# Graph convolution on one core: eight x quads loaded among the last segment's reads, and a table of gates for the scatters

## The chip, the cores and the metric

The kernel runs on one core of a Trainium2 chip. A core has TensorE (PE for its matmuls, PEld for its weight loads), VectorE (DVE), ScalarE (ACT), GpSimd (POOL) and SyncE (SP), which run side by side and wait for each other by semaphores, and 16 DMA engines that all queues share. Here SP issues the plain transfers and POOL the indirect ones, the scatters. The time is that of one execution on the device, in microseconds; lower is better.

## The reference

There are N = 12500 nodes with 128 features and 412500 edges (src, dst, 20 edge features, one weight), sorted by dst.

```python
h   = relu(layernorm(x)) @ W_in2f
Wij = (ssp(edge_attr @ W_f1 + b_f1) @ W_f2 + b_f2) * edge_weight[:, None]
agg = segment_sum(h[dst] * Wij, src, num_segments=N)     # ssp(x) = softplus(x) - log 2
out = x + ssp(agg @ W_o1 + b_o1) @ W_o2 + b_o2
```

The edges are sorted by the end that is read (dst), so the rows of h come from a narrow window; the sum goes by the other end (src), which is in random order.

## The kernel before

The edges are worked in 806 chunks of 512, that is four tiles of 128 edges each (`QT = 4`). A step of the main loop is one chunk, with the engines' parts of it staggered over several chunks. `hidden` (L710) multiplies the edge features by W_f1 on PE, ACT and DVE turn them into softplus values, `value` (L834) multiplies by W_f2 on PE, `window` and `pick` (L818, L846) pick the edges' rows of h out of their window by a 0/1 matrix, `blocks` and `rank` (L747, L766, L799, L771) work out a free slot for each edge, and `message` (L863, L864) writes the product and the edge's place in its node block into a buffer `o`. There are 16 such buffers (`BACK = 16`).

`scatter` (L873) then issues, on POOL, one indirect DMA for each of a chunk's four tiles, from `o` to a table `slots` in device memory. The chunks form seven segments, each with a table of its own. When a segment's chunks are scattered, `Collect` reads its table back (`load`, L919 on SP), compares places (`compare`, L932 on DVE, L938 on POOL), and sums by a matmul into `acc` (`add`, L953), and `keep` (L985, L987) adds `acc` to the nodes' sums `agg`. A unit is what one `load` reads. The first six segments' units are spread over later steps and over steps behind the last chunk; the seventh's are read at the end, together with the output stage `finish` (L443 to L460), which takes a quad (512 nodes) through two matmuls and adds x.

What sets the order: it is written out by hand, one queue per engine, in the order of the calls in `step(k, units)`. Three things tie the engines' paces. A buffer `o` is free again when its scatters of 16 chunks earlier have landed, so DVE's L863 waits for them. `behind` makes PE's matmuls of a step wait for the scatters of 16 chunks earlier. And `scatter(k, kept["v"])`, called behind `value(k + 1)`, gives the first scatter of chunk k-1 a wait for the last matmul of that `value`; this is the gate. Chunks before 24 (`PACED`) and the last 12 steps have no gate.

Of x, which `finish` adds to the result, 25 quads are loaded to SBUF ahead of the output stage. Eight come in the main loop (`x_early`). The other 17 (`x_late`: buffers xr, xf, xh and xm, 8, 4, 2 and 3 quads) are loaded on SP (L428) behind the sixth segment's last read and ahead of the seventh's first one, each with an addition of the bias on POOL (L433) that stands behind the last scatter.

Of the kernel before, what the change touches and what calls it, by code (L numbers as in the profile page):

```python
# [17 lines left out]
P = 128  # L18
# [27 lines left out]
def gnn_kernel(  # L46
# [498 lines left out]
    with tc.tile_pool(name="edge", bufs=2) as edge, tc.tile_pool(  # L545
# [57 lines left out]
        class Group:  # L603
# [101 lines left out]
            def hidden(self, c):  # L705

                z = psum.tile([P, 2, CH], F32, name="z")
                for k in range(2):
                    rows = slice(32 * (c + k), 32 * (c + k) + RBF)
                    mm = nc.tensor.matmul(z[:, k, :], wf1[rows, :], self.f[rows, :],  # L710
                                          start=True, stop=True)
                    if k == 1:
                        behind(mm, self.g * NCHUNK + c - LZ, 3)
                self.pair[c] = z

            def hidden_log(self, c):
# [36 lines left out]
            def rank(self, c):  # L753

                seg = self.seg
                if c == 0:
                    self.top = edge.tile([P, TG], F32, name="top")
                    self.slot = edge.tile([P, TG], I32, name="slot", bufs=8)
                k = self.g * NCHUNK + c
                if k > seg.c0:  # L760
                    self.pass_on()
                if k == seg.cleared and k > seg.c0:
                    used = self.used()
                    self.limit(6 * len(segs), ALU.is_gt, seg.low, used[:, :, :NBLK - 1])
                    self.limit(6 * len(segs) + 1, ALU.is_gt, seg.low_last, used[:, :, NBLK - 1:])
                nc.tensor.matmul(free, after, self.inb[c], start=k == seg.c0, stop=False,  # L766
                                 skip_group_check=True)
                kept["inb"] = self.inb[c]

            def rank_end(self, c):  # L770
# [58 lines left out]
            def value(self, c, v):  # L829

                r = self.pair[c // 2 * 2][:, c % 2, :]
                k = self.g * NCHUNK + c - 1
                for i in range(QT):
                    mm = nc.tensor.matmul(v[:, i, :], r[:, i * P:(i + 1) * P], wf2,  # L834
                                          start=False, stop=True, skip_group_check=True)
                    if i == 1:
                        behind(mm, k, k % 2)
                kept["v"] = mm
                return v

            def pick(self, c, at, ps):

                near = self.near.pop(c)
                k = self.g * NCHUNK + c - 2
                for i in range(QT):
                    mm = nc.tensor.matmul(ps[:, i, :], at[:, i * P:(i + 1) * P], near,  # L846
                                          start=i == 0, stop=i == QT - 1, skip_group_check=True)
                    if i == 1:
                        behind(mm, k, 2 + k % 2)

            def picked(self, c, ps):

# [11 lines left out]
                nc.vector.tensor_mul(o[:, :, :P], v, hg)  # L864
                self.o[c] = o

            def scatter(self, c, after=None):

                views = self.seg.views
                o = self.o.pop(c)  # L870
                for i in range(QT):
                    j = c * QT + i
                    put = nc.gpsimd.indirect_dma_start(  # L873
                        out=views[j % VIEWS],
# [2 lines left out]
                        in_offset=None,  # L877
                    )
                    puts.append(put.ins.name)
                    if i == 0 and after is not None:  # L880
# [13 lines left out]
        class Collect:  # L894
# [47 lines left out]
            def add(self, u):  # L942
                b0, nb, t0, nt = self.units[u]
                m, to = self.m.pop(u), self.to.pop(u)
                for j in range(nb * nt):
                    b, t = b0 + j // nt, t0 + j % nt
                    if b % QT == 0 and t == 0:
                        self.few = QT if "rest" in kept else 2
                    few = self.few
                    i = b % few  # L950
                    if i == 0 and t == 0:
                        self.acc[b // few] = self.room(b // few)
                    nc.tensor.matmul(self.acc[b // few][:, i, :], m[:, j, :P], to[:, j, :],  # L953
                                     start=t == 0, stop=t == self.seg.tiles(b) - 1)
# [93 lines left out]

        tops, ps = [], {}
        waiting = []  # L1050
        LAG, PACED = 1, 24

        def step(k, units=()):

# [11 lines left out]
            def message(k):  # L1066
                g, c = of(k)
                g.message(c, vs.pop(k), hgs.pop(k))
                waiting.append(k)
# [57 lines left out]
            for r in ready[-1:]:  # L1127
                next(r, None)
                tops.append(r)
            if k in HEAD:  # L1130
                part("end", made["log"] - 1, pairs(hidden_end))
            elif k != -1:
# [3 lines left out]
            for c, u in units:  # L1136
                if summed:
                    summed[0].add(summed[1])
                summed[:] = c, u

        zeros = {}
        units = {}
# [66 lines left out]
            return t.rearrange("p (c f) -> p c f", f=P)  # L1209

        xs = {}
        NX = 8

        def early_homes():
            for q in range(NX):
# [56 lines left out]
        with tc.manual_schedule():  # L1272
# [36 lines left out]
            x_late = x_ahead(late_homes(), nc.gpsimd, bo2)  # L1309
# [25 lines left out]
            nc.vector.tensor_copy(flag, worst)  # L1335
            for _ in x_early:
                pass
            for _ in x_late:
                pass


            last = collects[-1]
# [90 lines left out]
```

## Time and profile before

| | |
|---|---|
| median of 3 runs | 4208.53 us (4207.98 to 4208.92) |
| profiled execution | 4207.59 us, its span 4205.9 us |
| POOL busy in scatters | 3093.3 us, 3224 of 959 ns |
| POOL's idle time before scatters | 1011.8 us |
| first and last scatter start | 22.96 us, 4108.09 us |
| DVE's L863 waiting for scatters that land | 677.6 us |
| SP issues the 17 late quads of x | from 4100.85 us |
| SP issues the seventh segment's first read | 4119.62 us |
| DVE's first comparison of the seventh segment | 4123.84 us |

The profile names an operation by its line, engine and tiles (`out<-in`). Times of a timeline row are its start and its duration in us; in square brackets stands how long the engine was idle before it, and what ended that. In a group's row the numbers behind the bar are the sum of busy time in us, the mean duration of one in ns, and the idle time in front of them. "issue" is time in which an engine waited for nothing that the profile shows.

### The profile page before, as it was taken

To read this page: it belongs to the slowest core of one execution; us is meant where nothing else is said; L and a number is where in the kernel's file an instruction comes from. 1 tells how busy PE (TensorE), PEld (TensorE's weight loads), DVE (VectorE), ACT (ScalarE), POOL (GpSimd) and SP (SyncE) were. 2 spreads that over 40 slices of the span, in tenths; PEclk is the share of its full clock that TensorE was granted. 3 is DMA by queue.
4 is the path that set the end of the run, shared out by engine and by line. 5 is a ranking of instruction groups with operands and counts; after the bars stand their busy time and mean duration, and the time that the engine had idled before them with its cause. 6 is when DMAs were issued, how large, how long until landed. Compare 5 with 4: busy or idle time off the path is not lost. (4 is left out here: it accounts for less than half of the span.)

```text
span 4205.9 us, 68388 instructions
## 1 busy us (share of the span) xinstructions
PE 3305.9 (79%) x21594; PEld 2564.3 (61%) x21594; DVE 3134.5 (75%) x7192; ACT 2774.6 (66%) x5494; POOL 3137.6 (75%) x3298
## 2 busy tenths in 40 slices
PE   6777667676676666678888888988888888888887
PEld 4555445444444444457776776767777767667786
DVE  7887666666555555668877887888888888888986
ACT  6887676667666666666666666766666666666624
POOL 5777777777777777777777777777777777777774
PEclk8877776667766667679999998999999999999999
DMA  5776655655444354467778777778777977787776
GB/s 173 215 231 210 193 171 178 188 158 177 142 127 132 110 169 152 139 198 235 230 227 278 226 220 214 229 227 278 232 229 205 297 230 209 235 243 213 218 231 192
DMA packets 494767, 858.10 MB, mean 204 GB/s; under 512 B 141018, under 2 KB 276558, under 8 KB 494398
## 3 DMA queue, kind: packets, MB, share of 16 engines
q1 hardware_dynamic: 390798, 640.38, 52.1%
q0 software_dynamic: 103168, 213.15, 15.0%
q8 instruction: 174, 2.85, 0.3%
q14 instruction: 195, 1.60, 0.1%
q10 hardware_dynamic: 432, 0.13, 0.0%
HBM read 457.62 MB, written 395.69 MB: 203 GB/s over the span
## 5 line engine op out<-in xcount | busy, mean ns | idle before, releaser
L873 POOL DMA_INDIRECT slots<-o,slot x3224 | 3093.3, 959 | 1011.8 <-issue 720.4
L856 ACT ACTIVATE hg<-picked,rcut 128x128 f32<-128x128 f32 x3224 | 909.6, 364 | 409.5 <-PE picked L846 396.2
L834 PEld LDWEIGHTS v<-wf,r 128*128 128x128 f32 x6448 | 997.4, 233 | 252.4 <-issue 128.1
L834 PE MATMUL v<-wf,r 128*128 128x128 f32 x6448 | 1075.4, 321 | 24.2 <-ACT v L826 11.7
L953 PEld LDWEIGHTS acc<-to,m 128*128 128x128 f32 x5660 | 723.4, 205 | 213.4 <-DVE agg L987 87.6
L826 ACT ACTIVATE v<-bf 128x512 f32<-128x512 f32 x806 | 484.8, 601 | 535.2 <-DVE o L864 516.0
L710 PE MATMUL z<-f,wf 20*128 20x512 f32 x1612 | 564.5, 783 | 346.2 <-DVE r L742 343.9
L953 PE MATMUL acc<-to,m 128*128 128x128 f32 x5660 | 768.1, 293 | 71.0 <-DVE agg L987 51.1
L863 DVE COPY o<-place 128x4 f32<-128x4 f32 x806 | 151.8, 188 | 678.7 <-DMA slots<-o,slot 677.6
L932 DVE TENSOR_TENSOR to<-numbers,m 128x640 f32<-128x640 f32 (+3 forms) x793 | 629.7, 824 | 29.4 <-DMA m<-slots 19.7
L846 PE MATMUL picked<-near,at 126*128 126x128 bf16 x3224 | 363.7, 243 | 329.2 <-DVE o L864 322.8
L864 DVE TENSOR_TENSOR o<-v,hg 128x512 f32<-128x512 f32 x806 | 552.3, 685 | 80.3 <-PE v L834 75.1
L742 DVE SCALAR_TENSOR_TENSOR r<-z,nbf,a 128x1024 f32<-128x1024 f32 x402 | 512.8, 1276 | 81.3 <-ACT a L722 80.6
L846 PEld LDWEIGHTS <-at 126*128 126x128 bf16 x3224 | 290.5, 111 | 380.4 <-issue 310.7
L747 DVE TENSOR_TENSOR inb<-numbers,blk 128x392 f16<-128x392 f32 x806 | 446.1, 554 | 96.0 <-PE numbers L953 95.7
L719 ACT ACTIVATE a<-z,bf 128x1024 f32<-128x1024 f32 x402 | 442.4, 1101 | 113.8 <-PE z L710 113.5
L722 ACT ACTIVATE a<-a,half 128x1024 f32<-128x1024 f32 x402 | 461.6, 1148 | 13.1
L710 PEld LDWEIGHTS z<-f,wf 20*128 20x128 f32 x1612 | 142.3, 215 | 522.1 <-DVE r L742 493.2
L771 DVE TENSOR_REDUCE top<-free 128x4 f32<-128x392 f32 x806 | 446.1, 553 | 13.0 <-PE free L766 12.5
L720 ACT ACTIVATE a<-a 128x1024 f32<-128x1024 f32 x402 | 424.9, 1057 | 12.7
L953 PEld LDWEIGHTS numbers<-to,m 128*128 128x128 f32 x2492 | 326.7, 211 | 156.3 <-DVE to L932 145.2
L953 PE MATMUL numbers<-to,m 128*128 128x128 f32 x2492 | 354.9, 301 | 69.7 <-DVE to L932 68.8
(126 smaller groups left out, 1984.8 us busy)
## 6 DMA issues: line engine op xcount, KB each, us to landing
m<-slots SPq DMA_DIRECT2D x307, 387.0 KB
rel<-rel_d SPq DMA_DIRECT2D x202, 504.0 KB
m<-slots SPq DMA_DIRECT2D x278, 322.5 KB
f<-in_f_t SPq DMA_DIRECT2D x101, 512.0 KB
slots<-o,slot POOLq DMA_INDIRECT x3224
m<-slots SPq DMA_DIRECT2D x193, 258.0 KB
slots<-zero SPq DMA_DIRECT2D x96, 387.0 KB
slots<-zero SPq DMA_DIRECT2D x58, 516.0 KB
```

What stands on the lines that cost most here:

```text
L710: mm = nc.tensor.matmul(z[:, k, :], wf1[rows, :], self.f[rows, :], start=True, stop=True)
L722: nc.scalar.activation(a, a, AF.Ln, bias=half, scale=0.5)
L742: nc.vector.scalar_tensor_tensor(r, z, nbf1, a, op0=ALU.max, op1=ALU.add)
L747: nc.vector.tensor_tensor(inb, count_ps[:, None, :NBLK].to_broadcast([P, QT, NBLK]), self.blk[:, c * QT:(c + 1) * QT, None].to_broadcast([ ...
L826: nc.scalar.activation(v, spread(bf12, QT), AF.Copy)
L834: mm = nc.tensor.matmul(v[:, i, :], r[:, i * P:(i + 1) * P], wf2, start=False, stop=True, skip_group_check=True)
L846: mm = nc.tensor.matmul(ps[:, i, :], at[:, i * P:(i + 1) * P], near, start=i == 0, stop=i == QT - 1, skip_group_check=True)
L856: nc.scalar.activation(hg[:, i, :], ps[:, i, :], AF.Copy, scale=self.rcut[:, j:j + 1])
L864: nc.vector.tensor_mul(o[:, :, :P], v, hg)
L873: put = nc.gpsimd.indirect_dma_start(out=views[j % VIEWS], out_offset=bass.IndirectOffsetOnAxis(ap=self.slot[:, j:j + 1], axis=0), in_=o[: ...
L932: nc.vector.tensor_tensor(to[:, :n, :], count_ps[:, None, :].to_broadcast([P, n, P]), m[:, :n, P:].to_broadcast([P, n, P]), op=ALU.is_equal)
L953: nc.tensor.matmul(self.acc[b // few][:, i, :], m[:, j, :P], to[:, j, :], start=t == 0, stop=t == self.seg.tiles(b) - 1)
```

## The change

Three things are changed.

**The gates.** `STRETCH = 40` cuts the chunks into stretches of 40. For ten of the stretches a table `GATES` gives another gate than the one of before. `("v", 8)` and `("v", 12)` release two or three chunks' tiles together, at the `value` of a step one or two later. `("end", 4)` and `("end", 8)` release one or two chunks at the step's end, behind the last matmul that was issued in it, a collect's if there is one. `("each", 1)` releases one tile at each of four points of a step: behind `value`, `pick`, `rank` and at the end. To have that matmul, `kept["mm"]` takes each newest one. All other stretches gate as before.

**The front.** In stretches 12 and 16 (`FRONT`) the units' comparisons stand at the front of a step, ahead of `message`, and no longer behind `blocks`.

**The late x.** Nine of the 17 late quads are loaded and biased as before (`NOW = 9`: the eight xr and the first xf). The other eight (three xf, two xh, three xm, the last of them only 212 rows) are loaded on SP behind the seventh segment's reads of units 6, 8, 10 and so on, and get their bias on POOL three units later.

```diff
+        LAG, PACED, STRETCH = 1, 24, 40
+        GATES = {2: ("v", 2 * QT), 3: ("each", 1), 5: ("end", QT), 6: ("v", 3 * QT),
+                 7: ("v", 2 * QT),
...
+        FRONT = (12, 16)
...
-            def scatter(k, after=None):
-                while waiting and (waiting[0] < PACED or k >= NCH - PACED // 2
-                                   or after is not None and waiting[0] <= k - LAG):
-                    j = waiting.pop(0)
-                    g, c = of(j)
-                    g.scatter(c, after if j >= PACED and k < NCH - PACED // 2 else None)
-
+            def scatter(k, point=None):
+                while waiting:
+                    j, i = waiting[0]
+                    if j < PACED or k >= NCH - PACED // 2:
+                        n, after = QT - i, None
+                    else:
+                        where, n = GATES.get(j // STRETCH, ("v", QT))
+                        n = min(n, ((j // STRETCH + 1) * STRETCH - j) * QT - i)
+                        if point not in (("v", "pick", "rank", "end") if where == "each" else (where,)):
+                            return
+                        if j * QT + i + n > (k - LAG + 1) * QT:
+                            return
+                        after = kept["mm"]
+                    while n > 0:
+                        j, i = waiting.pop(0)
+                        g, c = of(j)
+                        e = min(QT, i + n)
+                        g.scatter(c, range(i, e), after)
+                        after = None
+                        n -= e - i
+                    if e < QT:
+                        waiting.insert(0, (j, e))
+                        return
+
+            front = 0 <= k < NCH and k // STRETCH in FRONT
+            for c, u in units if front else ():
+                c.compare(u)
             if k in vs:
                 message(k)
...
-                    scatter(k, kept["v"])
+                    scatter(k, "v")
...
                 g.pick(c, ats.pop(k + 2), ps[k + 2])
+                scatter(k, "pick")
...
             for c, u in units:
-                c.compare(u)
+                if not front:
+                    c.compare(u)
...
+            for w in late[:NOW]:
+                x_load(*w)
+            for w in late[:NOW]:
+                x_bias(*w, nc.gpsimd, bo2)
...
             for u in range(len(last.units)):
                 last.load(u + 5)
+                i = NOW + u // 2
+                if u % 2 and i < len(late):
+                    x_load(*late[i])
+                if not u % 2 and NOW <= i - 2 < len(late):
+                    x_bias(*late[i - 2], nc.gpsimd, bo2)
```

The order of the instructions shows the change at three places.

The SP queue behind the sixth segment's last read, before; `slots_122` is the seventh segment's table, and a row ends with the count of such instructions in a row:

```order
L428 DMA xr<-in_x 128x4x128 x8
L428 DMA xf<-in_x 128x4x128 x4
L428 DMA xh<-in_x 128x4x128 x2
L428 DMA xm<-in_x 128x4x128 x2
L428 DMA xm<-in_x 128x128
L428 DMA xm<-in_x 84x128
L919 DMA m<-slots_122 128x4x129 x8
```

The same place after:

```order
L428 DMA xr<-in_x 128x4x128 x8
L428 DMA xf<-in_x 128x4x128
L921 DMA m<-slots_122 128x4x129 x7
L428 DMA xf<-in_x 128x4x128
L921 DMA m<-slots_122 128x4x129 x2
L428 DMA xf<-in_x 128x4x128
```

The seventh segment's first read has moved up past nine x transfers (the last quad is two), and the moved ones stand between reads.

POOL in stretch 2, with what each scatter waits for, before (DMASW are the counters of the scatters' landings, eight in turn; DVE and PE those of the engines):

```order
L873 DMA slots_116<-o,slot 206848x129 [waits DMASW0_49,DVE_49,PE_49]
L873 DMA slots_116<-o,slot 206848x129 [waits DMASW1_49]
L873 DMA slots_116<-o,slot 206848x129 [waits DMASW2_49]
L873 DMA slots_116<-o,slot 206848x129 [waits DMASW3_49]
L873 DMA slots_116<-o,slot 206848x129 [waits DMASW4_49,DVE_49,PE_49]
```

After:

```order
L875 DMA slots_116<-o,slot 206848x129 [waits DMASW0_49,DVE_49,PE_49]
L875 DMA slots_116<-o,slot 206848x129 [waits DMASW1_49]
L875 DMA slots_116<-o,slot 206848x129 [waits DMASW2_49]
L875 DMA slots_116<-o,slot 206848x129 [waits DMASW3_49]
L875 DMA slots_116<-o,slot 206848x129 [waits DMASW4_49,DVE_49]
```

No scatter has moved; every second chunk's first scatter has lost its wait for PE, and the other's is for a later matmul.

DVE at the start of stretch 12, before (with the numbers of the buffers; L863 and L864 are `message`, L932 a comparison):

```order
L747 TENSOR_TENSOR inb_22500<-numbers_145,blk_22122 128x392
L932 TENSOR_TENSOR to_22502<-numbers_145,m_22357 128x640
L863 COPY o_22524<-place_22125 128x4
L864 TENSOR_TENSOR o_22524<-v_22440,hg_22478 128x4x128
L771 TENSOR_REDUCE top_22453<-free_144 128x4
L818 TENSOR_SCALAR at_22548<-rel_21825,prow_74 126x512
```

After:

```order
L748 TENSOR_TENSOR inb_22498<-numbers_145,blk_22120 128x392
L934 TENSOR_TENSOR to_22500<-numbers_145,m_22357 128x640
L934 TENSOR_TENSOR to_22524<-numbers_145,m_22411 128x768
L934 TENSOR_TENSOR to_22526<-numbers_145,m_22413 128x640
L865 COPY o_22528<-place_22123 128x4
L866 TENSOR_TENSOR o_22528<-v_22438,hg_22478 128x4x128
```

The comparisons of a step have moved up past its message, `rank_end`, `window` and `blocks`; at the stretch's first step two steps' comparisons meet.

More of the change, by code (lines that the diff above doesn't have):

```diff
@@ L765, in rank @@
                     self.limit(6 * len(segs) + 1, ALU.is_gt, seg.low_last, used[:, :, NBLK - 1:])
-                nc.tensor.matmul(free, after, self.inb[c], start=k == seg.c0, stop=False,
-                                 skip_group_check=True)
+                kept["mm"] = nc.tensor.matmul(free, after, self.inb[c], start=k == seg.c0,
+                                              stop=False, skip_group_check=True)
                 kept["inb"] = self.inb[c]
@@ L865, in message, with scatter @@
                 self.o[c] = o
-            def scatter(self, c, after=None):
+            def scatter(self, c, tiles, after=None):
                 views = self.seg.views
-                o = self.o.pop(c)
-                for i in range(QT):
+                o = self.o[c] if tiles[-1] < QT - 1 else self.o.pop(c)
+                for i in tiles:
                     j = c * QT + i
@@ L879, in scatter @@
                     puts.append(put.ins.name)
-                    if i == 0 and after is not None:
+                    if i == tiles[0] and after is not None:
                         tc.add_manual_dep(
@@ L952, in add @@
                         self.acc[b // few] = self.room(b // few)
-                    nc.tensor.matmul(self.acc[b // few][:, i, :], m[:, j, :P], to[:, j, :],
-                                     start=t == 0, stop=t == self.seg.tiles(b) - 1)
+                    kept["mm"] = nc.tensor.matmul(
+                        self.acc[b // few][:, i, :], m[:, j, :P], to[:, j, :],
+                        start=t == 0, stop=t == self.seg.tiles(b) - 1)
                     if t == self.seg.tiles(b) - 1 and (i == few - 1 or b == NBLK - 1):
@@ L1050, in gnn_kernel @@
         waiting = []
-        LAG, PACED = 1, 24
+        LAG, PACED, STRETCH = 1, 24, 40
+        GATES = {2: ("v", 2 * QT), 3: ("each", 1), 5: ("end", QT), 6: ("v", 3 * QT),
+                 7: ("v", 2 * QT),
+                 10: ("v", 2 * QT), 11: ("each", 1), 14: ("v", 2 * QT), 15: ("each", 1),
+                 18: ("end", 2 * QT)}
+        FRONT = (12, 16)
         def step(k, units=()):
@@ L1129, in step @@
                 tops.append(r)
+            scatter(k, "rank")
             if k in HEAD:
@@ L1139, in step @@
                 summed[:] = c, u
+            scatter(k, "end")
         zeros = {}
@@ L1211, in gnn_kernel @@
         xs = {}
-        NX = 8
+        NX, NOW = 8, 9
         def early_homes():
@@ L1337, in gnn_kernel @@
                 pass
-            for _ in x_late:
-                pass
+            late = []
+            for q, xo in late_homes():
+                xs[q] = xo
+                late.append((xo, x_pieces(q * QT, min(QT, NTILE - q * QT))))
+            for w in late[:NOW]:
+                x_load(*w)
+            for w in late[:NOW]:
+                x_bias(*w, nc.gpsimd, bo2)
             last = collects[-1]
```

7 lines of the change are left out of this document (4 added, 3 removed).

## The prediction, made before the changed kernel was run

> **What bounds the kernel now.** I read the page's table of engines and its costliest groups first, then the scatters' own line, then timelines of the start and the end.
>
> ```profile
> span 4205.9 us, 68388 instructions
> PE 3305.9 (79%) x21594; PEld 2564.3 (61%) x21594; DVE 3134.5 (75%) x7192; ACT 2774.6 (66%) x5494; POOL 3137.6 (75%) x3298
> L873 POOL DMA_INDIRECT slots<-o,slot x3224 | 3093.3, 959 | 1011.8 <-issue 720.4
> L873 POOL DMA_INDIRECT slots<-o,slot x3224: 952/958/1177, 23.0 to 4108.1; - x190
>   DVE o L863: 677.6, 285
> ```
>
> No engine is over 79% busy, but POOL's share is uneven in kind: 3093.3 us of scatters and 1011.8 us of gaps fill 4105.1 us, nearly all of the time up to the last scatter. The fourth line is the scatters' line: shortest, median and longest 952, 958 and 1177 ns. The fifth is from its list of who waited for it: DVE's L863, which needs a free `o`, 677.6 us. So DVE waits for POOL. The timeline shows what the gaps are.
>
> ```profile
> 57.98 0.96 POOL L873 DMA_INDIRECT slots<-o,slot  x1 [4.26 <-DVE o L864]
> 59.24 0.95 POOL L873 DMA_INDIRECT slots<-o,slot  x1 [0.30 <-issue]
> ...
> 4106.82 0.96 POOL L873 DMA_INDIRECT slots<-o,slot  x1 [0.30 <-issue]
> 4108.09 0.95 POOL L873 DMA_INDIRECT slots<-o,slot  x1 [0.30 <-issue]
> ```
>
> The row at 57.98 is the last with a real wait. From 59.24 to 4108.09, 4048.85 us, the 3224 less 21 earlier scatters follow each other every 1.264 us, 0.96 of work and 0.30 of gap, whatever the gate. The main loop is POOL's queue, and only two things could change it: the length of a scatter, or a gate that binds.
>
> Behind the last scatter stands the tail:
>
> ```profile
> 4100.85 9.33 SPq L428 DMA_DIRECT2D xr<-in_x  x8
> 4110.22 4.22 SPq L428 DMA_DIRECT2D xf<-in_x  x4
> 4114.53 1.65 SPq L428 DMA_DIRECT2D xh<-in_x  x2
> 4116.23 3.02 SPq L428 DMA_DIRECT2D xm<-in_x  x4
> 4119.62 4.91 SPq L919 DMA_DIRECT2D m<-slots  x7
> ...
> 4109.06 9.79 POOL L433 TENSOR_TENSOR xr<-xr,bo 128x512 f32<-128x512 f32 x8
> 4123.84 0.69 DVE L932 TENSOR_TENSOR to<-numbers,m 128x512 f32<-128x512 f32 x1 [12.40 <-DMA m<-slots]
> 4124.63 4.54 PE L953 MATMUL acc<-to,m 128*128 128x128 f32 x24 [13.93 <-DVE to L932]
> 4130.07 0.69 ACT L446 ACTIVATE a_out<-z_out,bo 128x512 f32<-128x512 f32 x1 [86.28 <-PE z_out L443]
> 4145.51 0.69 ACT L446 ACTIVATE a_out<-z_out,bo 128x512 f32<-128x512 f32 x1 [0.58 <-PE z_out L443]
> 4148.21 0.69 ACT L446 ACTIVATE a_out<-z_out,bo 128x512 f32<-128x512 f32 x1 [0.60 <-PE z_out L443]
> 4198.14 2.57 SPq L460 DMA_DIRECT2D out<-xm  x4
> ```
>
> SP issues 18 x transfers (17 quads) from 4100.85 to 4119.25, and only then the seventh segment's first read. DVE idles 12.40 us and PE 13.93 for it. Then the output runs at 2.70 us a quad (4145.51 to 4148.21), the chain of PE, ACT and DVE, and ends with the last stores.
>
> **The late x, the term that counts.** The DMA engines in this stretch:
>
> ```profile
> DMA packets 14601, 8.92 MB, mean 297 GB/s; under 512 B 650, under 2 KB 14443, under 8 KB 14599
> q0 software_dynamic: 96, 0.19, 16.2%
> q0 software_dynamic: 1, 0.00, 0.1%
> 4100.00:4124.00 24.00, 9.68 (x80) 8.94 (x78) 8.73 (x15) 0.00 (x0) 21.84 (x21) 0.80 1.11 314
> 4130.00:4140.00 10.00, 9.24 (x58) 7.06 (x57) 5.96 (x10) 8.04 (x12) 3.06 (x6) 1.00 0.39 97
> 4140.00:4180.00 40.00, 40.00 (x271) 32.97 (x270) 33.49 (x54) 30.59 (x45) 17.49 (x31) 1.00 0.73 198
> ```
>
> The first line is 4100 to 4130 us, the next two are the scatters' queue at 4109 to 4113 and at 4113 to 4114 (one packet, the last of all), the last three the windows of the tail; their last two numbers are the DMA engines' share and GB/s. The DMA engines are full until 4124 and have room afterwards (0.39, then 0.73). Eight quads moved are seven of 256 KB and 106 KB, 1.94 MB, and at 297 GB/s that is 6.5 us which no longer passes ahead of the first read. Three prices for the gain of the first comparison:
> - From below: the read needs the last scatter landed, at latest 4114.0. Before, the comparison began 4.22 us behind the issue (4123.84 - 4119.62); so 4118.2, a gain of 5.6 us.
> - By the data that passes ahead: 6.5 us.
> - From above: SP is done with its ninth transfer at about 4111.3 (4110.22 and a quarter of 4.22); a read issued then would gain 4119.62 - 4111.3 = 8.3 us.
>
> I take 6.6: the DMA engines are full there, so it is nearest to the data. DVE, PE and the output stage behind the first comparison all hang on it in the same order, and shift with it.
>
> What the moved loads cost later: each stands on SP behind a read, takes 0.8 to 1.1 us of the queue (4.22 for 4), and SP has only a read and a store of 0.4 to 0.5 us per quad of 2.70 us. The first of them stands behind unit 6's read, five units ahead of its use. For the DMA engines it is 256 KB in 5.4 us, 48 GB/s more on 198, about 0.18 on a share of 0.73. If that cover were gone, a read would be late by the 0.9 us of one x quad, with four units or 10 us of lead. On POOL the eight biases move from idle time into the rows below:
>
> ```profile
> L433 POOL TENSOR_TENSOR xf<-xf,bo 128x512 f32<-128x512 f32 x4 | 4.9, 1250 | 0.0
> 4145.94 2.33 POOL L938 TENSOR_SCALAR to<-places,m 128x128 f32<-128x128 f32 x4 [4.33 <-DMA m<-slots]
> 4151.34 2.33 POOL L938 TENSOR_SCALAR to<-places,m 128x128 f32<-128x128 f32 x4 [3.06 <-DMA m<-slots]
> ```
>
> A bias (1.25) and a comparison (2.33) are 3.6 us in a round of 5.40: nothing. Quad 17, the first whose x comes late, is added some 46 us (17 x 2.70) after the first read.
>
> The Trainium skill, page "DMA: Bandwidth & Descriptors", section "Where 436 GB/s comes from", puts the limit between device memory and a core at about 358 GB/s; by it the 1.94 MB would be 5.4 us, an estimate, and the sum 1.2 us less of a gain. The measured 297 GB/s, with full engines and packets of 611 bytes on average (8.92 MB by 14601), stands here, so I keep 6.6.
>
> **The gates.** What a gate can cost depends on how far PE is ahead. These are `value`'s matmuls (eight to a chunk) and the scatters (four to a chunk) up to 640 and up to 3877 us:
>
> ```profile
> L834 PE MATMUL v<-wf,r x1088: 271/377/583, 18.3 to 638.1; 128*128 128x128 f32 x182
> L873 POOL DMA_INDIRECT slots<-o,slot x480: 952/958/1177, 23.0 to 639.1; - x160
> L834 PE MATMUL v<-wf,r x6200: 271/275/583, 18.3 to 3873.6; 128*128 128x128 f32 x194
> L873 POOL DMA_INDIRECT slots<-o,slot x3041: 952/958/1177, 23.0 to 3876.8; - x191
> ```
>
> 136 chunks against 120, and 775 against 760: PE is 15 to 16 chunks ahead. The gate of before asks for two, the strictest new one (12 tiles) for four, the step's end for at most one more. None of them ever waits, so behind POOL's queue nobody waits either. The waits themselves: with three of them or one, the gap is 0.30 us in every row. Cost 0.
>
> What is left is the length of a scatter. All time above the median is 3093.3 - 3224 x 0.958 = 4.7 us for the whole kernel. The change touches 12 of 20 stretches: it can gain at most 2.8 us. It can lose if the scatters meet DVE differently; within a stretch of before the longest is 1051 ns:
>
> ```profile
> L873 POOL DMA_INDIRECT slots<-o,slot x162: 954/958/1051, 639.1 to 842.7; - x162
> ```
>
> so a step that is always hit costs 0.09 us and a stretch of 40 such steps 3.7 us. As gates that never wait don't move DVE, I take a gain of 0.5, near nothing.
>
> **The front.** It moves 40 steps' comparisons in each of two stretches ahead of `message`. DVE there waits for a free `o` anyway, and `o` is 15 chunks ahead of POOL; if a comparison waits for its read, the message is late by that, and the scatter 70 us later isn't. Cost 0; the worst is one comparison more, once at a stretch's start (0.69 us in the tail's row).
>
> **The sum.** 4207.59 (the profiled execution) - 6.6 - 0.5 = 4200.5. The median of the runs shown is 0.94 us above that execution, so 4201.4 is the forecast, 0.17% faster. A measurement here tells about 0.2% or 8.4 us from no change; the border is 4200.1.
>
> **The rivals.**
> - *The tail gains more.* The first read follows SP's ninth transfer (8.3 us), PE is slowed for a shorter time (24 matmuls of the first three units take 4.54 us, where 3 x 1.06 at the later rate would be 3.2), and the 2.8 us of stretched scatters go. 8.3 + 1.4 + 2.8 is 12.5: 4196. For it: SP's queue is what stands between 4111.3 and 4119.62. Against it: full DMA engines, and the last scatter at 4113 to 4114. A part of it is enough for 4200.
> - *The late x collides with the reads*, and the change doesn't do what it says. If the output's first quads were bound by DMA, the 6.6 us would come back there: 4208. Against it the shares of 0.39 and 0.73.
> - *Scatters get longer*, the slower side. A DVE phase that hits one scatter in every step costs 3.7 us a stretch; with five of the 12 stretches fully hit, 18.5 us, the sum is slower by over 0.2% (4208.5 - 7.1 + 18.5 = 4220), and the break-even lies at two. For it: the steps are locked to POOL's beat through `o`, so a bad phase would stay. The Trainium skill, page "SBUF — State Buffer", section "Who interferes with whom", says that GpSimd and certain DVE operations lock each other out for a whole instruction; the trace has a median of 958 against a shortest of 952, so little of it here.
> - *A gate binds.* Price, by the row at 57.98: up to 4.26 us per group of scatters, 20 groups in a stretch of 8-tile groups, 85 us: 4290. It needs PE less than four chunks ahead instead of 15.
>
> **Chances.** The forecast 0.60, more gain 0.24, collision 0.07, longer scatters 0.06, a binding gate 0.03. The forecast's own range is 4199.5 to 4203. The range of 8 in 10 leaves out the two slow cases and the far end of the gain: 4196.5 to 4207. Faster by over 0.2% takes the second case and a tenth of the first: 0.30; slower 0.09; within 0.2% the rest, 0.61.
>
> **What would show it.** Scatters that still start every 1.264 us with 0.30 of gap, the last at 4107.5 to 4108.5; no wait above 0.5 behind 58 us. SP's first read of the seventh segment at 4113 to 4115, DVE's first comparison near 4117 with some 6 us idle before it instead of 12.40, the first `a_out` near 4123.4, the output still at 2.70 us a quad, the DMA share over 0.39 in the 10 us behind it. The prediction is wrong if POOL waits for PE, if scatters' mean leaves 959 by more than 1 ns, or if the quads' pace grows beyond 2.75.

## The result

| | before | after |
|---|---|---|
| median of 20 runs | 4208.73 us (4205.96 to 4212.39) | 4203.67 us (4201.1 to 4208.22) |
| ratio to before | | 0.9987, interval 0.9981 to 0.9993 |
| profiled execution, its span | 4207.59, 4205.9 us | 4201.87, 4200.2 us |
| last scatter starts | 4108.09 us | 4108.54 us |
| from there to the seventh segment's first read | 11.53 us | 5.46 us |
| from there to the first comparison | 15.75 us | 9.68 us |
| from there to the end | 97.8 us | 91.7 us |

The kernel is 0.13% faster, 5.1 us, within the 0.2% that one measurement resolves; over 20 runs the interval still excludes no gain. In the profiles all of it is in the tail. The timeline of after, at the place where the prediction quoted the one of before:

```profile
4103.56 8.00 SPq L428 DMA_DIRECT2D xr<-in_x  x8
...
4107.28 0.96 POOL L875 DMA_INDIRECT slots<-o,slot  x1 [0.31 <-issue]
4108.54 0.96 POOL L875 DMA_INDIRECT slots<-o,slot  x1 [0.30 <-issue]
...
4111.61 0.95 SPq L428 DMA_DIRECT2D xf<-in_x  x1
4114.00 5.07 SPq L921 DMA_DIRECT2D m<-slots  x7
4118.22 0.69 DVE L934 TENSOR_TENSOR to<-numbers,m 128x512 f32<-128x512 f32 x1 [5.22 <-DMA m<-slots]
...
4124.45 0.69 ACT L446 ACTIVATE a_out<-z_out,bo 128x512 f32<-128x512 f32 x1 [78.96 <-PE z_out L443]
...
4129.13 0.69 ACT L446 ACTIVATE a_out<-z_out,bo 128x512 f32<-128x512 f32 x1 [0.59 <-PE z_out L443]
4131.82 0.69 ACT L446 ACTIVATE a_out<-z_out,bo 128x512 f32<-128x512 f32 x1 [0.59 <-PE z_out L443]
```

SP has nine x loads behind it and issues the first read at 4114.00 instead of 4119.62. The comparison follows 4.22 us later, the same as before, and so starts 5.62 us earlier in the span (4123.84 to 4118.22). `a_out` shifts by the same 5.62 (4130.07 to 4124.45), the output still goes at 2.69 us a quad, and the span ends 5.7 us earlier.

What held the read until 4114.00 is seen in the scatters' DMA queue; its rows for 4112 to 4113.1 and for 4113.1 to 4114 (packets, MB, share of the DMA engines):

```profile
q0 software_dynamic: 4, 0.01, 2.5%
...
q0 software_dynamic: 1, 0.00, 0.1%
```

The last packet of the last scatter still passes behind 4113.1. SP is done with its ninth load at 4112.56 (4111.61 + 0.95) and then waits 1.44 us. The trace's record of the last scatter's landing stands at 4113.86, 5.32 us behind its start, and the read goes out 0.14 us later. So in after the read follows the last scatter and no longer SP's list.

The eight loads that moved cost nothing later. The windows of the tail (the last two numbers are the DMA engines' share and GB/s) and two of POOL's rows:

```profile
4130.00:4140.00 10.00, 10.00 (x67) 8.07 (x67) 8.35 (x14) 7.43 (x12) 5.75 (x8) 1.00 0.48 133
4140.00:4180.00 40.00, 40.00 (x275) 33.26 (x274) 33.50 (x53) 30.49 (x45) 20.86 (x33) 1.00 0.75 208
```

```profile
4127.30 1.27 POOL L433 TENSOR_TENSOR xf<-xf,bo 128x512 f32<-128x512 f32 x1 [1.54 <-PE acc L955]
4128.55 2.35 POOL L940 TENSOR_SCALAR to<-places,m 128x128 f32<-128x128 f32 x4
```

The share rises from 0.39 to 0.48 and from 0.73 to 0.75; a bias and a comparison fit into a round on POOL.

The loop gained nothing. The scatters' group on the page of after, and the longest waits of DVE in stretch 12 (2461 to 2663 us), where the comparisons are in front, first of before and then of after:

```profile
L875 POOL DMA_INDIRECT slots<-o,slot x3224 | 3094.4, 960 | 1011.2 <-issue 686.1
```

```profile
DVE o L863 <- DMA slots<-o,slot: 12.0, 9, 2.7
```

```profile
DVE to L934 <- PE numbers L955: 48.2, 12, 6.6
```

3094.4 us of scatters against 3093.3, 1011.2 of gaps against 1011.8; the last scatter starts 0.45 us later. But the last row is new: in front of the step DVE waits 12 times, 48.2 us in all, for PE's additions (L955) in `numbers`. That is paid out of PE's lead over POOL. `value`'s matmuls (eight a chunk) and scatters (four) of after, up to 2400 and up to 2661 us:

```profile
L835 PE MATMUL v<-wf,r x3864: 271/275/583, 18.4 to 2400.0; 128*128 128x128 f32 x194
L875 POOL DMA_INDIRECT slots<-o,slot x1872: 954/958/1177, 23.2 to 2399.1; - x188
...
L835 PE MATMUL v<-wf,r x4224: 271/275/583, 18.4 to 2659.6; 128*128 128x128 f32 x192
L875 POOL DMA_INDIRECT slots<-o,slot x2079: 954/958/1177, 23.2 to 2660.8; - x189
```

483 chunks against 468 is a lead of 15. At the end of stretch 12 it is 528 against 519.75, some 8. The front was free because the stretch ended before the lead did; two stretches later the lead is back at 14 to 16.

### The profile page after: what moved, and what is told of

Read it like the earlier page. It is cut to its first block, busy times and chain, and to the rows that moved or that the text cites. A ratio compares the mean times of both kernels' runs of the same rounds, so it can differ in the third digit from the quotient of the medians.

```text
span 4200.2 us, 68754 instructions
## 1 busy us (share of the span) xinstructions
PE 3295.7 (78%) x21594; PEld 2560.0 (61%) x21594; DVE 3128.5 (74%) x7192; ACT 2775.2 (66%) x5494; POOL 3139.1 (75%) x3298
## 5 line engine op out<-in xcount | busy, mean ns | idle before, releaser
L875 POOL DMA_INDIRECT slots<-o,slot x3224 | 3094.4, 960 | 1011.2 <-issue 686.1
L835 PEld LDWEIGHTS v<-wf,r 128*128 128x128 f32 x6448 | 985.5, 230 | 250.5 <-issue 133.1
L835 PE MATMUL v<-wf,r 128*128 128x128 f32 x6448 | 1064.0, 318 | 22.7 <-ACT v L827 12.3
L955 PEld LDWEIGHTS acc<-to,m 128*128 128x128 f32 x5660 | 727.1, 206 | 192.0 <-DVE agg L990 77.0
L955 PE MATMUL acc<-to,m 128*128 128x128 f32 x5660 | 769.9, 294 | 54.6 <-DVE agg L990 43.6
L955 PEld LDWEIGHTS numbers<-to,m 128*128 128x128 f32 x2492 | 330.7, 213 | 152.0 <-DVE to L934 113.6
L955 PE MATMUL numbers<-to,m 128*128 128x128 f32 x2492 | 359.1, 303 | 63.8 <-DVE to L934 55.7
```

Of the source, the lines that this page charges most:

```text
L875: put = nc.gpsimd.indirect_dma_start(out=views[j % VIEWS], out_offset=bass.IndirectOffsetOnAxis(ap=self.slot[:, j:j + 1], axis=0), in_=o[: ...
L955: kept["mm"] = nc.tensor.matmul(self.acc[b // few][:, i, :], m[:, j, :P], to[:, j, :], start=t == 0, stop=t == self.seg.tiles(b) - 1)
```

## The experiments

They ran on three chips. On the first, before takes 4208.11 us (median of 27 runs), as in the result. On the second it takes 5039.14 and on the third 5025.66. So each ratio is to before's runs on the same chip, and times are compared within a chip, or it is said that they aren't.

My theory was: the gain is the late x alone; gates and front are free as long as PE is far ahead. The rival was that gates and front move the loop as well, to either side, and that the sum hides it.

**The parts alone (first chip).** The late x without gates and front, the gates and the front without the late x, and the late x with no gate at all:

```diff
late_x_alone:
-        GATES = {2: ("v", 2 * QT), 3: ("each", 1), ...
-        FRONT = (12, 16)
+        GATES = {}
+        FRONT = ()

gates_and_front_alone:
-        NX, NOW = 8, 9
+        NX, NOW = 8, 17

no_gate (as late_x_alone, and):
-        LAG, PACED, STRETCH = 1, 24, 40
+        LAG, PACED, STRETCH = 1, NCH, 40
```

> The eight late quads alone: the gates and the order of DVE are those of before. If the late x carries the whole change, the first comparison of the seventh segment starts 5 to 6 us earlier than before's 4123.84, as it did with everything on (4118.22), and the time is 0.11 to 0.15% under before. If the gates carry part of it, this gains under 4 us; if they cost something, it gains 6.5 us or more.

> The ten gates and the two stretches with comparisons in front, with all 17 late quads ahead of the reads as before. If gates that never wait do nothing, the time is before's within 1.5 us, the scatters start every 1.264 to 1.265 us, and their mean length stays at 959 to 960 ns. If they cost what was missing of the forecast, it is 1 to 2 us slower; if they gain, 1 to 3 us faster.

> Late x as changed, no scatter waits for PE at all, comparisons as before. If no gate ever waits, taking all of them away changes nothing: the time of late x alone within 1.5 us, scatters every 1.264 to 1.265 us. If the gate of before holds scatters off bad moments of DVE, the scatters' mean goes over 962 ns and the time is 10 us or more above late x alone.

| | median, runs | ratio, interval |
|---|---|---|
| late x alone | 4203.56 us, 11 | 0.9989, 0.9980 to 0.9998 |
| gates and front alone | 4207.73 us, 11 | 1.0000, 0.9991 to 1.0009 |
| late x, no gate | 4202.90 us, 11 | 0.9988, 0.9979 to 0.9997 |

The late x is the whole gain; the gates and the front give nothing; and neither does the gate of before, since without any gate the time is the same. In the tail of late_x_alone the first comparison starts 4.95 us before the 4123.84 of before, just short of the 5 to 6 that I expected, behind a last scatter that starts 1.98 us later than before's:

```profile
4110.07 0.95 POOL L875 DMA_INDIRECT slots<-o,slot  x1 [0.30 <-issue]
...
4116.03 4.08 SPq L921 DMA_DIRECT2D m<-slots  x7
4118.89 0.69 DVE L934 TENSOR_TENSOR to<-numbers,m 128x512 f32<-128x512 f32 x1 [8.25 <-DMA m<-slots]
```

There SP is free from 4110.75 on (its ninth load is the row "4109.84 0.91"), 5.3 us before it issues the read. What SP waits for in that time, and the last window before the read (the last two numbers are the DMA engines' share and GB/s):

```profile
SPq L921 <- DMA slots<-o,slot: 5.0, 4, 1.7
```

```profile
4115.00:4116.00 1.00, 0.00 (x0) 0.00 (x0) 0.00 (x0) 0.00 (x0) 1.00 (x2) 0.50 0.03 7
```

The x loads have passed, SP is free and the DMA engines are all but idle, and still the read waits. The last scatter's landing is recorded 5.81 us behind its start, the read goes out at 5.96; in no_gate these are 5.50 and 5.64, in after 5.32 and 5.46. That settles which of the prediction's three prices limits the read: the landing of the last scatter, not SP's list and not the data of x. With the engines idle the first comparison follows after 2.86 us instead of 4.22, but the output doesn't gain by it: PE's first 24 additions take 5.46 us there and 4.54 in after, and the first `a_out` comes 15.97 us behind the last scatter's start, 15.91 in after.

**Quarters and the front in every stretch (first chip).**

```diff
-        GATES = {2: ("v", 2 * QT), 3: ("each", 1), ...
-        FRONT = (12, 16)
+        GATES = dict.fromkeys(range(21), ("each", 1))
+        FRONT = range(21)
```

> Late x as changed, and every stretch has the gate of one tile at each of four points of the step and the comparisons in front. If neither matters, the time is that of late x alone within 1.5 us and the mean scatter 959 to 961 ns. If the finer gates or the front make scatters meet DVE more often, the effect of the changed stretches is seen nearly twofold here: a mean over 961 ns, 3 us or more.

4493.85 us over 5 runs, ratio 1.0675 (1.0660 to 1.0689). Its stretches 11 and 12 in the windows view (us; then PE, PEld, DVE, ACT and POOL), its waits, and its lead at 2690 us:

```profile
2259.30:2461.40 202.10, 168.80 (x1193) 139.11 (x1191) 143.24 (x293) 122.18 (x246) 153.31 (x161) 0.89 0.75 237
2461.40:2690.60 229.20, 188.00 (x1289) 154.41 (x1288) 158.20 (x330) 131.04 (x264) 153.28 (x160) 0.87 0.64 194
```

```profile
DVE to L934 <- PE numbers L955: 519.6, 161, 6.7
...
POOL slots L875 <- PE acc L955: 158.3, 126, 7.3
```

```profile
L835 PE MATMUL v<-wf,r x4184: 271/275/583, 18.3 to 2689.9; 128*128 128x128 f32 x200
L875 POOL DMA_INDIRECT slots<-o,slot x2080: 952/958/1232, 23.0 to 2688.9; - x190
```

Neither expectation was right: the time is 290 us above late_x_alone's, and the scatters are no longer than they were. POOL's 160 scatters take the same 153.3 us in both stretches, but the second stretch is 27 us longer: the lead is down to 523 less 520, three chunks, and POOL now waits for PE. The first comparisons come at the end of stretch 8, the lead falls behind it, and the time grows from the moment the lead is used up. This run can't tell the front from the quarters.

**Gate or front, and which resource (second chip).** The front everywhere with the gates of before; the same with one more buffer `to`; the same with the comparison reading `places`, which lies in SBUF, in place of its copy in `numbers`, a PSUM tile in which PE also accumulates; and, without a front, a gate of 15 chunks, as much as the lead on the first chip.

```diff
front_everywhere:
+        GATES = {}
+        FRONT = range(21)

front_everywhere_one_more_to (as front_everywhere, and):
-                to = edge.tile([P, UT, P], F32, name="to", bufs=5)
+                to = edge.tile([P, UT, P], F32, name="to", bufs=6)

front_everywhere_places (as front_everywhere, and):
-                                            count_ps[:, None, :].to_broadcast([P, n, P]),
+                                            places[:, None, :].to_broadcast([P, n, P]),

gate_fifteen_chunks (GATES = {}, FRONT = (), and):
-                        where, n = GATES.get(j // STRETCH, ("v", QT))
+                        where, n = GATES.get(j // STRETCH, ("v", 15 * QT))
```

> Late x as changed, every chunk gated as before, comparisons in front in all stretches. If the front alone made the 290 us of the run with both, the time is 4450 to 4510 and DVE waits some 500 us in its comparisons for PE's L955. If it takes the finer gates too, the front alone stays near 4204 and only DVE's and PE's lead over the scatters shrinks.

> As the run with the front everywhere, with six buffers of the comparisons' result `to` for five. If a comparison in front waits because its buffer is still read by the sum of five units earlier, a sixth buffer takes away most of the wait: under 100 us of it are left and the time falls by 100 us or more. If it waits because it reads the bank `numbers`, into which PE has just summed, the buffer changes nothing: within 20 us of the front everywhere.

> As the run with the front everywhere, but the comparison on DVE reads the same numbers from `places` in SBUF and not from the bank `numbers` in PSUM. If the wait comes from that bank, it is gone: DVE's wait for L955 in front of comparisons under 50 us, and the time is within 10 us of late x alone, or above it by what the comparison gets slower. If it comes from the buffers of `to`, nothing changes.

> Late x as changed, comparisons as before, and every stretch releases 15 chunks together (15, 15 and 10 in a stretch of 40), so that the first of them needs PE 16 chunks ahead of the scatters. PE's lead is 13 to 15 chunks, so this gate must bind where the changed kernel's (two to four chunks) doesn't: POOL idle for PE of 3 to 9 us per group, some 55 groups, 150 to 500 us slower. If the time stays, the lead was not what kept the gates of the change from costing anything.

| | median, runs | ratio, interval |
|---|---|---|
| front everywhere | 5308.61 us, 2 | 1.0536, 1.0497 to 1.0574 |
| one more `to` | 5297.25 us, 2 | 1.0513, 1.0453 to 1.0574 |
| comparing with `places` | 4999.91 us, 3 | 0.9916, 0.9892 to 0.9939 |
| gate of 15 chunks | 7247.72 us, 2 | 1.4384, 1.4331 to 1.4438 |

A free `to` is not what the comparison waits for. Reading `places` takes the loss away, so the cause of the loss is the shared tile: the comparison reads a constant in `numbers`, and is held until PE's additions in the same tile are done. That the ratio comes out under 1 is more than the loss taken away; how much of it is the late x and how much is `places` itself, no run separates. DVE's wait in front_everywhere, its scatters in stretch 9, and those of front_everywhere_places in the same stretch (us, then POOL's busy time and count):

```profile
DVE to L934 <- PE numbers L955: 349.0, 86, 7.2
```

```profile
2145.10:2414.20 269.10, 153.25 (x160) 0.80 0.53 166
```

```profile
2135.70:2374.10 238.40, 162.89 (x160) 0.84 0.60 187
```

With `places` 5.1 us of the comparison's waits named `numbers` are left of 349.0, and the stretch is 31 us shorter, although a scatter then takes 1.02 us (162.89 by 160) instead of 0.96. The Trainium skill, page "SBUF — State Buffer", section "Who interferes with whom", says that a DVE instruction with two SBUF inputs contends with a GpSimd instruction that reads SBUF. Scatters that grow by 6% beside comparisons with both inputs in SBUF agree with it. On the first chip, where POOL's queue is the bound, the longer scatters would probably stand in the time; that was not run.

The gate of 15 shows what a gate does that binds. POOL's largest sum of waits is

```profile
POOL slots L875 <- PE picked L847: 2520.6, 48, 82.4
```

48 waits, 53 us each on average and up to 82.4. I had expected 3 to 9 us a group and 150 to 500 us in all, and the run is 2200 us slower: the price of such a gate was off by far. The run can't tell at which width a gate starts to bind on the first chip, as the lead is another on this one (below).

**How many quads ahead of the read (third chip).** After's kernel with 5, none and 13 quads ahead instead of 9; and the front everywhere once more, with 9.

```diff
late_x_five_ahead, late_x_thirteen_ahead, all_late_x_among_reads:
-        NX, NOW = 8, 9
+        NX, NOW = 8, 5        (13; 0)

all_late_x_among_reads, one load per unit instead of every other unit:
-                i = NOW + u // 2
-                if u % 2 and i < len(late):
-                    x_load(*late[i])
-                if not u % 2 and NOW <= i - 2 < len(late):
-                    x_bias(*late[i - 2], nc.gpsimd, bo2)
+                if u and NOW + u - 1 < len(late):
+                    x_load(*late[NOW + u - 1])
+                if NOW <= NOW + u - 4 < len(late):
+                    x_bias(*late[NOW + u - 4], nc.gpsimd, bo2)
```

> After's kernel with 5 quads of x ahead of the first read instead of 9 (12 among the reads instead of 8). Counted from the start of the last scatter, after issues its first read at +5.46, compares first at +9.68 and ends at +91.62. Theory (the last scatter's landing is the bound, and x ahead of it delays both the landing and the read): the landing comes at +3.9 to +4.3 (it is +3.90 where no x is near it), the read goes out within 0.8 of it, and with less x before it the comparison follows after about 3 us instead of 4.22: +7.5 to +8.5, end at +89.5 to +90.5, ratio to before 0.998. Rival 1, the landing is as late however little x is ahead: end at +91 to +92. Rival 2, data that passes ahead sets it (0.85 us a quad): end at +88.2. Rival 3, the twelve loads collide with reads and stores: the output slower than 2.75 us a quad and the end later than +91.6.

> After's kernel with none of the 17 quads of x ahead of the first read: one load per unit from unit 1 on, its bias four units' loads later. Landing theory: landing at +3.9, first read at +4.3 to +4.8, comparison at +7 to +7.5, end at +88.5 to +89.5; hardly less than with five ahead. Rival, data ahead sets it: nine quads of 0.85 us, end at +84. Collision: a read, a store and an x load for each 2.70 us are 770 KB or 285 GB/s, nearly the 297 that the full DMA engines moved before, so from unit 7 to 17 the output may run above 2.75 us a quad; ten quads by 0.2 us take the gain back, end at +91.

> After's kernel with 13 quads ahead and 4 among the reads: halfway between before and after. If each quad that passes ahead costs its data (0.85 us), the first read and the end come 3.4 us later than in after: read at +8.9, comparison at +13, end at +95. If only SP's ninth transfer or the landing counted, the cost of the tenth to thirteenth would be the same, since they stand behind both; a smaller loss (end at +93) would say that something else than data ahead limits.

> The comparisons in front in all stretches, scatters gated as before, late x as in after: the run that showed 1.054 on a chip where the loop is slow anyway. Theory (the comparison waits for PE's last sums in the bank that it shares with them, so each step in front eats some of PE's lead until 3 chunks are left): the loss shows here too, ratio 1.03 to 1.07, DVE L934 waiting for PE numbers for some 500 us, lead down to 3 by about stretch 12. Rival (the loss with each gate and the front together came from the gates at a quarter's grain, and the front costs nothing): 0.998 to 1.001.

| | median, runs | ratio, interval |
|---|---|---|
| five ahead | 5110.02 us, 5 | 1.0176, 1.0153 to 1.0198 |
| none ahead | 5111.00 us, 5 | 1.0177, 1.0158 to 1.0195 |
| thirteen ahead | 5129.53 us, 4 | 1.0206, 1.0186 to 1.0226 |
| front everywhere, nine ahead | 5297.77 us, 2 | 1.0538, 1.0514 to 1.0562 |

On this chip the tail starts otherwise: the last scatter has landed long before SP gets to the seventh segment's reads, since PE and DVE are still adding the sixth: with five ahead the last scatter starts at 4960.29 and the first read goes out at 5019.71. So the expected times behind the last scatter can't be judged, and whether five or none ahead would beat after on the first chip stays open. What can be judged is the data. DVE's first comparison of the seventh segment, with 13 quads ahead, with 9 (this row is of front_everywhere_again), with 5 and with none:

```profile
5046.61 0.69 DVE L934 TENSOR_TENSOR to<-numbers,m 128x512 f32<-128x512 f32 x1 [8.41 <-DMA m<-slots]
```

```profile
5218.93 0.69 DVE L934 TENSOR_TENSOR to<-numbers,m 128x512 f32<-128x512 f32 x1 [4.20 <-DMA m<-slots]
```

```profile
5024.83 0.69 DVE L934 TENSOR_TENSOR to<-numbers,m 128x512 f32<-128x512 f32 x1 [0.92 <-DMA m<-slots]
```

```profile
5026.51 2.46 DVE L934 TENSOR_TENSOR to<-numbers,m 128x512 f32<-128x512 f32 x4
...
5036.36 0.69 ACT L446 ACTIVATE a_out<-z_out,bo 128x512 f32<-128x512 f32 x1 [0.59 <-PE z_out L443]
5039.05 0.69 ACT L446 ACTIVATE a_out<-z_out,bo 128x512 f32<-128x512 f32 x1 [0.59 <-PE z_out L443]
```

The idle time falls from 8.41 to 4.20 to 0.92 us, 1.05 and 0.82 us for each quad taken out, about the 0.88 us that a quad takes at the prediction's 297 GB/s. These are single executions; with nine ahead the same row of front_everywhere on the second chip has 4.93. With none ahead it is gone, and the output goes at 2.69 us a quad even while an x load stands behind every read: the collision that both the prediction and these expectations feared doesn't happen. Five and none ahead end alike, since nothing is left to remove. The front everywhere repeats the second chip's 1.0536; its gates are those of before, so the front costs without the quarters.

The larger finding is the ratio: a change that gains 0.13% on the first chip loses 1.8 to 2.1% here in three variants that have its gates and its front and differ from it only in the number of quads ahead. After itself did not run here. Five stretches, 9 to 13, of late_x_five_ahead (us, then POOL's busy time and count), and the lead at 2382 us:

```profile
2142.00:2382.80 240.80, 153.90 (x160) 0.86 0.60 187
2382.80:2641.10 258.30, 153.92 (x160) 0.84 0.60 177
2641.10:2878.90 237.80, 153.73 (x160) 0.87 0.68 215
2878.90:3142.80 263.90, 153.88 (x161) 0.84 0.57 171
3142.80:3389.50 246.70, 154.01 (x161) 0.87 0.59 180
```

```profile
L835 PE MATMUL v<-wf,r x3229: 269/421/583, 18.3 to 2381.9; 128*128 128x128 f32 x190
L875 POOL DMA_INDIRECT slots<-o,slot x1600: 955/962/1178, 23.0 to 2376.3; - x178
```

403.6 chunks against 400: PE is under four chunks ahead. Counted over the whole trace, it is 3 to 6 chunks ahead in stretches 1 to 18. Stretch 9 has the gate of before, 10 the gate of two chunks, 11 quarters, 12 the front, 13 the gate of before. Against the two with the gate of before, the gate of two chunks costs 12 to 18 us and the front 17 to 23; quarters cost nothing.

Later stretches grow by themselves: 17, with the gate of before, takes 256.4 us. So for the whole sum I take the same stretches of front_everywhere_places, which has the gate of before everywhere and almost no wait for `numbers`. Stretches 10, 12, 14 and 16 (two chunks, front, two chunks, front) take 258.3, 263.9, 254.1 and 271.7 us here against 238.8, 239.8, 239.9 and 241.6 there, 88 us in all, and the median is 84.4 us above before's (5110.02 - 5025.66). That is an estimate, as the two runs are from two chips and no trace of before exists on either. A small lead alone is not enough for a gate to cost: stretches 2 and 7 have the same gate of two chunks with 3 to 6 chunks of lead, ahead of the first comparisons, and take 232.0 and 230.5 us, where stretches 4 and 8 with the gate of before take 233.6 and 231.4.

## Why the prediction was right or wrong

- **The main loop is POOL's queue, and the gates and the front don't move it.** Right on the first chip: the gates and the front alone are 1.0000, no gate at all changes nothing. The 0.5 us that I took for shorter scatters has nothing behind it. The profile of after has 1.1 us more of scatters and its last one 0.45 us later, but the profiles of one chip differ by more than that from execution to execution (last section), so the sign isn't shown either.
- **The late x, 6.6 us.** The mechanism was right, the size was off. From the last scatter's start the comparison gained 6.07 us (15.75 to 9.68), less the 0.45 us of the later scatter 5.62. Of the three prices the one from below, 5.6 us from the landing of the last scatter, is the one that decides, and I took it for a bound that the data would pass. The row was there: the scatters' queue still held a packet at 4113 to 4114. That the price came out to the hundredth is partly luck: it used the 4.22 us from the read's issue to the comparison, which were 4.22 again in after, but 2.86 in late_x_alone and 4.30 in no_gate.
- **The data price** of 297 GB/s, about 0.88 us a quad, was about right where the landing doesn't stand in the way: 0.82 and 1.05 us a quad on the third chip.
- **What the moved loads cost later: nothing.** Right: 2.69 us a quad, DMA shares of 0.48 and 0.75, and the same pace with twice as many loads among the reads.
- **The front costs 0.** The time came out right, by luck as far as the reasoning goes. I looked for a late read; what makes DVE wait is PE's additions in the tile that holds the comparison's constant. It took 7 of 15 chunks of lead in one stretch of 40 steps. "The worst is one comparison more" is refuted: 27 us in stretch 12 of each_and_front_everywhere, when the lead is gone.
- **The rivals.** The tail gained less, not more, and nothing collided with the reads. Scatters grew by 0.3 ns on average (3093.3 and 3094.4 us, by 3224), within the spread of executions. A gate that binds was given 0.03 with a condition, PE less than four chunks ahead. On the first chip the lead is 8 chunks at the least in the changed stretches, so this rival had no ground there. On the third, with 3 to 6, the gate of two chunks costs 12 to 18 us in a stretch by the rows above, and not the 85 that the rival took; and the front costs too, which no rival had.
- **The sum.** 4207.59 - 5.62 - 0.1 behind the first comparison is the 4201.87 of the profiled execution, against 4200.5 forecast. The median of 20 runs lies 1.8 us above that execution, not 0.94; together 2.3 us above the forecast of 4201.4. At 4203.67 the median lies 0.7 us outside the forecast's own range, 4199.5 to 4203, and inside the range of 8 in 10.

## What to carry to other kernels

When a read is moved ahead of other transfers, look at what it waits for itself: here the last scatter's landing left 5.6 us to gain, where the data moved out of its way would have given 6.5 and SP's queue 8.3. The landing isn't quite fixed: in each_and_front_everywhere, where no x load is near, it is recorded 4.28 us behind the last scatter's start instead of 5.32, so by these two numbers fewer quads ahead may gain up to another microsecond on the first chip; that is an estimate and was not run. "Never waits" is a statement about a reserve: count how far ahead the other engine is, and ask whether the edit eats of it; the same gates and front are free with some 15 chunks of lead, and by the estimate above they are the 1.8% that is lost with 3 to 6. A constant that is read from a PSUM tile in which matmuls still accumulate put its readers behind those matmuls here; before a reader is moved to an earlier place, look at everything else that lives in its tile.

## What the runs showed of the hardware

First, kernels were not equally fast on all chips: before takes 4208 us on one, 5039 and 5026 on the two others. The single instructions of POOL and DVE are hardly slower: in the third chip's run of late_x_five_ahead the scatters are 954/962/1178 ns (shortest, median, longest), in after 954/958/1177, and DVE is busy 3148.4 us against 3128.5. PE is busy for longer, 3612.5 us against 3295.7, and the granted TensorE clock is lower over the span. The views of cores, of after on the first chip and of late_x_five_ahead on the third:

```profile
core 0: 4200.2 us, clock 0.844
```

```profile
core 0: 5106.6 us, clock 0.781
```

What lies behind it stays open. The rows of waits don't tell: the traces of the second and third chip hold a third to a half of the semaphore records of the first chip's (33,014 of the engines' in late_x_five_ahead, 101,536 in after), so many waits there have no cause in the records, and sums by cause are probably too small. The 349.0 and 5.1 us of front_everywhere and front_everywhere_places are of two such traces, with 35,642 and 31,379 records; the lengths of their stretches don't rest on these records. The tail shows none of the slowness: in late_x_five_ahead the output goes at the same 2.69 us a quad.

Second, one kernel's executions on the first chip differ by up to 7 us (4200.72 to 4207.86 for no_gate), and the scatters account for most of what the profiles show of it: 3224 of them took 3094.4 us in after's profile (4201.87 us) and 3099.8 us in that of no_gate (its slowest execution, 4207.86 us), and likewise 3093.3 us in before's (4207.59 us) and 3099.6 us in that of gates_and_front_alone (4212.80 us). Nearly 2 ns a scatter is 5.4 us of a time. Each pair is of two kernels whose medians differ by 1 us at most; no kernel has two profiles.
